# Value matrices dealt out between score products, and the next batch's right factors put behind a pair's additions

## The chip, the cores and the metric

The kernel runs on one core of one Trainium2 chip. The metric is the time of one execution in microseconds (us) on the device, as the median of several runs. A profile of one further execution shows each engine's instructions: TensorE (PE, with its weight loads as PEld), VectorE (DVE), ScalarE (ACT), GpSimd (POOL) and the queue of SyncE (SP), which issues most of the transfers.

## What is computed

A gated block of cross attention and feed-forward, in float32. `x` is 4 x 1024 x 512, the context 4 x 64 x 512; 16 heads of 64.

```python
def _L0_xattn_ref(query, key, value, w_q, w_k, w_v, w_o):
    q = split_heads(query @ w_q)
    k = split_heads(key @ w_k)
    v = split_heads(value @ w_v)
    scores = jnp.einsum('bhqd,bhkd->bhqk', q, k) * SCALE
    mask = (k_pos[None, :] <= q_pos[:, None])
    scores = scores + (1.0 - mask)[None, None, :, :] * -10000.0
    weights = jax.nn.softmax(scores, axis=-1)
    out = jnp.einsum('bhqk,bhkd->bhqd', weights, v)
    return out.transpose(0, 2, 1, 3).reshape(...) @ w_o

x = x + tanh(g_xattn) * _L0_xattn_ref(_layernorm(x), ctx, ctx, w_q, w_k, w_v, w_o)
x = x + tanh(g_ffn) * _L0_ffn_ref(_layernorm(x), w_gate, w_up, w_down)
```

The feed-forward part (`_L0_ffn_ref`) multiplies by weights of 4 bits and quantizes its activations to 16 bits; it follows the attention in the kernel, and the change does not touch it.

## The kernel before

**Tiling.** The 4096 tokens are 32 tiles of 128 rows. Two tiles make a *pair* q, so there are 16 pairs, four for each of the four batches. The kernel folds weights together ahead of the pairs. For each batch, `m_all[b]` is w_q times the batch's keys, 512 x 1024 (two parts), so that scores are one matrix product of the normalized tokens with `m_all[b]`. The *value matrix* `vwo[b]` is the batch's values times w_o times tanh(g_xattn), 1024 x 512 (two parts of four head pairs), so that the attention's output is one product of the softmax weights with `vwo[b]`.

**Seven products.** A pair's scores, and its attention, are each computed as a 2 x 2 block product with seven block products in place of eight. This needs sums of blocks of the left operand (for scores: `score_left`, four DVE additions on `xs`; for attention: the end of `weights_turned`, four on `eT`), and sums of blocks of the right operand: `batch_sums(b, k)`, four DVE operations of 128 x 1024, with k = 0 for the scores (`m_all`) and k = 1 for the attention (`vwo`). `batch_sums` is a generator with a `yield` after the second and after the fourth operation. The results of the seven products are added together from the PSUM banks by DVE and ACT.

**Stages up to the pairs.** In the first block (pool `su`, five PSUM banks `ps_mm`), keys are projected, then for each of eight head pairs `hp` w_q is turned and `m_all` made (L478 to L505), with the value projection in every second step (L507). The statistics of the first layer norm are taken there too. In the last of the eight steps the left factors of pair 0 are made (L482: `centred`, which normalizes two tiles on ACT as `xn`, and `score_left`, which transposes them on PE, copies them to `xs` on ACT and adds on DVE). Then comes the value stage (L527 to L547): 32 value matrices of 128 x 512, eight for each batch, each from two matmuls of 64 x 64 against 512 columns into one bank, and each scaled out of PSUM, by ACT for batches 0 and 2 (L543) and by DVE for 1 and 3 (L545). Batches 2 and 3 come first and are written to DRAM by POOL's queue (L547), since the 20 shared buffers `slot` cannot hold everything; between the two halves stands `batch_sums(0, 0)`.

**The pairs.** In the second block (three banks `ps_s` for scores, two `ps_o` for the attention, three `ps_tr` for transposes), L731 to L734 make pair 0's scores (`scores(0)`, with pair 1's left factors after its sixth product), its softmax and `batch_sums(0, 1)`. Each step q of the loop at L735 then makes the scores of pair q + 1, with calls put between the seven products (`between`, keyed by the product's number; the products run in the order 1, 6, 2, 5, 7, 3, 4), then softmax of pair q + 1, and last the attention of pair q (`attend`, products in the order 1, 6, 2, 7, 5, 4, 3). One `turn()` transposes the softmax weights of one of pair q's two tiles; for pair 0 both turns stand after the whole of pair 1's scores and softmax (L758), for later pairs they stand between the score products. After `attend`, in the second and fourth pair of a batch, the right factors of the next batch are made (L777), then norms (L782 to L788), and one or two weight blocks of the feed-forward are dequantized (L791).

**What sets the order.** In the second block, PE's instructions are issued in the order of the program (`manual_schedule`, L553). All other engines, and PE in the first block, follow an order made ahead of the run by a list scheduler: it takes the operation that is earliest in the program among those that it reckons to be ready by its own costs, and `high_priority(SOON)` moves an operation 150 places forward. So an operation late in the program can run early if its engine is reckoned free, and one early in the program goes first where both are ready. The order is fixed when the program is built; in the run each engine goes through its list.

Of the kernel before, what the change touches and what calls it, by code (L numbers as in the profile page):

```python
# [7 lines left out]
F32 = mybir.dt.float32  # L8
# [3 lines left out]
AF = mybir.ActivationFunctionType  # L12
# [5 lines left out]
P = 128  # L18
# [9 lines left out]
def kernel(  # L28
# [335 lines left out]
    def batch_sums(b, k):  # L364
# [21 lines left out]
        nc.vector.tensor_tensor(t4, b21, t2, sub)  # L386
        yield

    with tc.tile_pool(name="su", bufs=1) as su, tc.tile_pool(
        name="ps_mm", bufs=5, space=PSUM  # L390
    ) as ps_mm:
# [86 lines left out]
        for hp in range(HP):  # L478
            if hp + 1 < HP:
                query_turned(hp + 1)  # L480
            else:
                left[0] = score_left(0, centred(0))  # L482
            for h2 in range(HC // 2):
                two = [
                    ps_mm.tile([P, 2, CT], F32, name=f"ps_m{hp}_{h2}_{j}", tag="mm")
                    for j in range(2)
                ]
                for i in range(2):
                    hc = 2 * h2 + i
                    for j in range(2):  # L490
                        half = slice(j * D, (j + 1) * D)
                        nc.tensor.matmul(
                            two[j][:, i, :],
                            wqT[hp // 4][half, hp % 4, hc * P : (hc + 1) * P], kT[half, hp, :],
                            start=True, stop=True,
                        )
                for j in range(2):
                    for b in range(B):
                        at = (hp % 4) * P + (j if b % 2 == 0 else 1 - j) * D
                        dst = m_all[b][hp // 4][:, 2 * h2 : 2 * h2 + 2, at : at + D]  # L500
                        src = two[j][:, :, b * KL : (b + 1) * KL]
# [18 lines left out]
            for k in range(2):  # L520
                nc.gpsimd.dma_start(out=m_d[b][k], in_=m_all[b][k])


        for b in range(B):
            vwo.append([slot([P, HP // 2, H], f"vwo{b}_{n}") for n in range(2)])
        load_group(1)
        for a in reversed(range(B // 2)):  # L527
            if a == 0:
                for _ in batch_sums(0, 0):
                    pass  # L530
            for hp in range(HP):
                for b in (2 * a, 2 * a + 1):
                    ps = ps_mm.tile([P, H], F32, name=f"ps_vo{b}_{hp}", tag="mm")
                    for j in range(2):
                        half = slice(j * D, (j + 1) * D)
                        to = j if b % 2 == 0 else 1 - j
                        nc.tensor.matmul(
                            ps[to * D : (to + 1) * D, :], vT[half, hp, b * KL : (b + 1) * KL],
                            wo[hp // 4][half, hp % 4, :], start=True, stop=True,
                        )  # L540
                    dst = vwo[b][hp // 4][:, hp % 4, :]
                    if b % 2 == 0:
                        nc.scalar.activation(dst, ps, AF.Copy, scale=tanh_g[0])  # L543
                    else:
                        nc.vector.tensor_scalar(dst, ps, tanh_g[0], None, ALU.mult)  # L545
                    if b > 1 and hp % 4 == 3:
                        nc.gpsimd.dma_start(out=vwo_d[b][hp // 4], in_=vwo[b][hp // 4])  # L547


    xT = [None] * NTB  # L550
    with tc.tile_pool(name="ps_s", bufs=1, space=PSUM) as ps_s, tc.tile_pool(
        name="ps_o", bufs=1, space=PSUM
    ) as ps_o, tc.manual_schedule(engines={mybir.EngineType.PE}):  # L553

        def scores(q, between):

            a, b = left.pop(q), right[0][q // QPB]
            e = pa.tile([P, 2, NH, KL], F32, name=f"e{q}", tag="e")
            c = e.rearrange("p i (n h) k -> p i n (h k)", n=2)
            bank = {  # L560
                k: ps_s.tile([P, H], F32, name=f"{k}{q}", tag=k) for k in ("sp", "sq", "sn")
            }
            m1, c12, c22 = c[:, 1, 0], c[:, 0, 1], c[:, 1, 1]
            for k, at, start, dst, other in (
                (1, "sp", True, m1, None), (6, "sq", True, c12, m1), (2, "sp", False, c[:, 0, 0], None),
                (5, "sn", True, c22, m1), (7, "sq", False, c22, c22), (3, "sn", False, c12, c12),
                (4, "sq", False, m1, m1),
            ):
                for h in range(HC // 2):
                    nc.tensor.matmul(  # L570
                        bank[at], a[k][:, h, :], b[k][:, h, :],
                        start=start and h == 0, stop=h == HC // 2 - 1, skip_group_check=True,
                    )
                with tc.high_priority(SOON):
                    if other is None:
                        nc.scalar.copy(dst, bank[at])
                    else:
                        nc.vector.tensor_tensor(dst, bank[at], other, add)
                if k in between:
                    between[k]()  # L580
            return e

        def softmax(q, e):

            for i in range(2):
                t = 2 * q + i
                ei = e[:, i]

                if t % TPB == 0:
                    nc.vector.tensor_tensor(  # L590
                        ei, ei, cmask.unsqueeze(1).to_broadcast([P, NH, KL]), ALU.add
                    )
                mx = pa.tile([P, NH], F32, name=f"mx{t}", tag="mx")
                nc.vector.tensor_reduce(mx, ei, AX.X, ALU.max)
                sm = pa.tile([P, NH], F32, name=f"sm{t}", tag="sm")
                if q == 0:

                    nc.vector.tensor_tensor(
                        ei, ei, mx.unsqueeze(2).to_broadcast([P, NH, KL]), ALU.subtract
                    )  # L600
                    nc.scalar.activation(ei, ei, AF.Exp)
                    nc.vector.tensor_reduce(sm, ei, AX.X, ALU.add)
                else:
                    nc.vector.tensor_scalar(mx, mx, -1.0, None, ALU.mult)  # L604
                    for h in range(NH):
                        nc.scalar.activation(  # L606
                            ei[:, h, :], ei[:, h, :], AF.Exp, bias=mx[:, h : h + 1],
                            accum_out=sm[:, h : h + 1],
                        )
                rs = pa.tile([P, NH], F32, name=f"rs{t}", tag="rs")  # L610
                nc.vector.reciprocal(rs, sm)
                nc.vector.tensor_tensor(
                    ei, ei, rs.unsqueeze(2).to_broadcast([P, NH, KL]), ALU.mult
                )

        def weights_turned(q, e):

# [21 lines left out]
        def attend(q, a):  # L639
# [15 lines left out]
            for k, at, start, dst in (  # L655
# [9 lines left out]
                with tc.high_priority(SOON):  # L665
                    if k == 1:
                        nc.scalar.copy(r, bank[at])
                    else:
                        nc.vector.tensor_tensor(dst, bank[at], dst, add)  # L669

                if k == 6:
                    nc.vector.tensor_tensor(x1[:, RIGHT], x1[:, RIGHT], r, add)
# [832 lines left out]
```

## Time and profile before

| | |
|---|---|
| median of the runs shown (3 runs, 1468.91 to 1469.15) | 1469.0 us |
| the profiled execution, whole | 1467.07 us |
| its span in the profile | 1465.3 us |
| first score product of pair 0 starts | 82.06 us |
| attention of pair 0 ends, scores of pair 2 start | 130.93 us |
| attention of the last pair (15) ends | 551.37 us |
| granted PE clock over the span | 0.995 |

A row of the timeline gives the start and the length in us, the engine, the line of the program, the operation, the tile that is written and those that are read, the shape, the count of merged instructions, and in brackets the idle time of the engine before it and who ended it. One matmul in float32 appears as two records, so a score product of two matmuls is `x4` and an attention product of four is `x8`. Rows of PE overlap by some 0.2 us; the distance of two starts is what a product takes. The tile names are the program's: `xn` and `xs` for left factors of scores, `e` for scores and softmax weights, `eT` for turned weights, `sp`, `sq`, `sn` and `opn`, `oq` for banks, `xg` for a group of four token tiles to which the attention is added in place, `vb` and `mb` for a batch's value and score matrices fetched back from DRAM.

### The profile page before, as it was taken

How to read it: one execution, taken by the hardware profiler on the slowest of the kernel's cores; microseconds unless marked ns; L12 is line 12 of the kernel's file. 1: busy time of each engine (PE TensorE's matmuls, PEld its weight loads, DVE VectorE, ACT ScalarE, POOL GpSimd, SP SyncE). 2: the span in 40 equal slices, each digit the busy share in tenths (PEclk: the TensorE clock that was granted, in tenths of full speed). 3: DMA queues.
4: the chain of work that ended last, by engine and by line, in shares of the span. 5: the costliest groups of instructions: out<-in, count | busy, mean ns of one | idle time of the engine just before them, and what ended most of it. 6: DMA issues, size and time to landing. Idle time of an engine off the chain costs nothing. (4 is left out here: it accounts for less than half of the span.)

```text
span 1465.3 us, 15463 instructions
## 1 busy us (share of the span) xinstructions
PE 1417.2 (97%) x5040; PEld 869.3 (59%) x5040; DVE 1128.0 (77%) x2059; ACT 693.4 (47%) x1746; POOL 96.6 (7%) x191
## 2 busy tenths in 40 slices
PE   8898999999999998999999999999999899999999
PEld 6545766766676674444444444444444448888887
DVE  2976887977988779899956569988888897666632
ACT  2645867767678673111000049977776532222200
POOL 0100000000000001000000000000000101111110
PEclk9999999999999999999999999999999999999999
DMA  9630231431312133664322439958557475554321
GB/s 330 244 130 15 72 115 72 159 129 58 130 47 110 46 130 158 236 223 187 129 86 102 157 127 345 373 216 316 212 210 267 164 282 174 187 187 172 143 72 43
DMA packets 74168, 240.12 MB, mean 164 GB/s; under 512 B 7396, under 2 KB 7652, under 8 KB 68068
## 3 DMA queue, kind: packets, MB, share of 16 engines
q1 hardware_dynamic: 48612, 137.39, 26.8%
q0 software_dynamic: 18560, 76.56, 13.4%
q10 hardware_dynamic: 6912, 25.17, 4.3%
q8 instruction: 39, 0.64, 0.2%
q14 instruction: 45, 0.37, 0.1%
HBM read 130.03 MB, written 109.05 MB: 163 GB/s over the span
## 5 line engine op out<-in xcount | busy, mean ns | idle before, releaser
L606 ACT ACTIVATE e<-e,mx 128x64 f32<-128x64 f32 x480 | 159.7, 339 | 2.2 <-DVE mx L604 2.1
L839 PE MATMUL pqup<-t,wuT 128*128 128x512 f32 x192 | 92.3, 603 | 5.2 <-DVE raw_up L860 2.6
L606 ACT ACTIVATION_READ_ACCUMULATOR e<-e,mx 128x1 f32 x480 | 92.3, 192 | 0.0
L839 PE MATMUL pqgate<-t,wgT 128*128 128x512 f32 x192 | 90.2, 592 | 0.0
L855 ACT COPY raw_gate<-ppgate 128x512 f32<-128x512 f32 x24 | 14.0, 585 | 145.5 <-PE ppgate L839 145.5
L1372 PE MATMUL ep<-wdT,upe 128*128 128x256 f32 x336 | 77.1, 379 | 0.0
L1298 ACT ACTIVATE uie<-upe,inv_up 128x1024 int16<-128x1024 f32 x48 | 53.8, 1145 | 45.8 <-DVE upe L1302 28.7
L661 PE MATMUL oq<-t,eT 128*128 128x256 f32 x256 | 63.7, 393 | 12.0 <-DVE xg L669 8.1
L1372 PE MATMUL eq<-tw,upe 128*128 128x256 f32 x312 | 72.4, 379 | 0.0
L1372 PEld LDWEIGHTS ep<-wdT,upe 128*128 128x128 f32 x336 | 63.8, 190 | 9.1 <-issue 0.5
L1071 ACT ACTIVATE gi<-gt,inv_gate 128x1024 int16<-128x1024 f32 x48 | 54.9, 1143 | 30.3 <-DVE q L1081 30.0
L839 PEld LDWEIGHTS pqup<-t,wuT 128*128 128x128 f32 x192 | 34.7, 189 | 57.0 <-issue 29.7
L839 PE MATMUL ppgate<-xh,wgT 128*128 128x512 f32 x144 | 67.7, 592 | 0.0
L839 PE MATMUL ppup<-xu,wuT 128*128 128x512 f32 x144 | 67.7, 592 | 0.0
L1372 PEld LDWEIGHTS eq<-tw,upe 128*128 128x128 f32 x312 | 59.3, 190 | 8.1
L839 PEld LDWEIGHTS pqgate<-t,wgT 128*128 128x128 f32 x192 | 36.3, 190 | 46.1 <-issue 37.9
L1302 DVE SCALAR_TENSOR_TENSOR upe<-uie,inv_o,gse 128x1024 f32<-128x1024 int16 (+1 forms) x50 | 60.4, 1231 | 3.3 <-ACT uie L1298 3.0
L661 PEld LDWEIGHTS oq<-t,eT 128*128 128x128 f32 x256 | 49.4, 195 | 21.9 <-DVE xg L669 11.0
L570 PE MATMUL sq<-t,xs 128*128 128x512 f32 x128 | 60.3, 593 | 0.0
L629 ACT COPY eT<-ps_e 128x512 f32<-128x512 f32 x64 | 34.3, 588 | 53.5 <-PE ps_e L627 53.5
L967 DVE TENSOR_REDUCE am_gate<-raw_gate 128x1 f32<-128x1024 f32 x48 | 58.2, 1213 | 0.9
L1103 ACT ACTIVATE ar<-raw_up 128x1024 f32<-128x1024 f32 x46 | 48.2, 1047 | 19.1 <-DVE raw_up L1029 19.1
(353 smaller groups left out, 3141.2 us busy)
## 6 DMA issues: line engine op xcount, KB each, us to landing
gate_d<-raw_gate ACTq DMA_DIRECT2D x48, 512.0 KB, 2.6
gt<-gate_d SPq DMA_DIRECT2D x48, 512.0 KB, 4.8
upe<-up_d SPq DMA_DIRECT2D x24, 1024.0 KB, 5.9
up_d<-raw_up POOLq DMA_DIRECT2D x46, 512.0 KB, 3.5
gse<-gsi_d SPq DMA_DIRECT2D x24, 512.0 KB, 4.6
gsi_d<-q SPq DMA_DIRECT2D x44, 256.0 KB, 4.0
xg<-in_x_dram SPq DMA_DIRECT2D x8, 1024.0 KB, 5.2
x_d<-xg POOLq DMA_DIRECT2D x32, 256.0 KB, 2.3
```

Source lines behind the costliest of these rows:

```text
L570: nc.tensor.matmul(bank[at], a[k][:, h, :], b[k][:, h, :], start=start and h == 0, stop=h == HC // 2 - 1, skip_group_check=True,)
L606: nc.scalar.activation(ei[:, h, :], ei[:, h, :], AF.Exp, bias=mx[:, h : h + 1], accum_out=sm[:, h : h + 1],)
L629: nc.scalar.copy(eT[:, 2 * i + k], ps)
L661: nc.tensor.matmul(bank[at], a[k][:, h, :], b[k][:, h, :], start=start and h == 0, stop=h == HP // 2 - 1, skip_group_check=True,)
L839: nc.tensor.matmul(bank[at], a[k][:, h, :], b[k][:, h, :], start=start and h == 0, stop=h == HC // 2 - 1, skip_group_check=True,)
L855: nc.scalar.copy(r0[:, 0, :], bank["pp"])
L967: nc.vector.tensor_reduce(am_gate[:, u : u + 1], rf, AX.X, ALU.max, apply_absolute_value=True)
L1071: nc.scalar.activation(gi, g, AF.Copy, scale=inv_g)
L1103: nc.scalar.activation(ar, raw[u], AF.Abs)
L1298: nc.scalar.activation(ui, up[:, i, :], AF.Copy, scale=inv_u)
L1302: ins = nc.vector.scalar_tensor_tensor(o[:, i, w], ui[:, w], c_o, gs[:, i, w], ALU.mult, ALU.mult)
L1372: nc.tensor.matmul(bank[at], a[u // 2][k][:, u % 2, q % 2, :], w_of[u // 2][k][:, u % 2, :], start=start and u == 0, stop=u == UPB - 1, sk ...
```

## The change

Three things are done.

1. **Value stage.** Only batches 2 and 3 are made there, in one loop over head pairs; ACT evicts twelve of the sixteen matrices and DVE four. `batch_sums(0, 0)` now stands ahead of that loop, and pair 0's left factors in it (at `hp == 2`) rather than in the last projection step.
2. **Pairs 0 and 1.** The eight value matrices of batch 0 are made two at a time after the products 6, 2, 5 and 7 of `scores(0)`; those of batch 1 after the products 1, 6, 2 and 5 of `scores(1)`. They use the two banks of `ps_o`, and ACT evicts all of them. Pair 1's left factors (`next_left(1)`) move from between the products of `scores(0)` to after `softmax(0)`. `batch_sums(0, 1)` is split: its first two operations stand before `softmax(0)`, its last two after `softmax(1)`. Pair 0's two turns move from after `softmax(1)` to after the products 3 and 4 of `scores(1)`, and pair 2's left factors from after product 3 to after product 4.
3. **Later batches.** `attend` returns its last addition, and the four operations of `batch_sums(b + 1, ...)` in the pairs 1, 3, 5, 7, 9 and 11 are placed on DVE's list behind it (`issue_after`).

`scores` and `softmax` move out of the second block with their bodies as they were, but that `scores` gets its three banks as an argument.

```diff
@@ L386: moved here from the second block @@
+    def scores(q, between, banks):
...
+        bank = dict(zip(("sp", "sq", "sn"), banks))
...
@@ L478, in the last projection step @@
             if hp + 1 < HP:
                 query_turned(hp + 1)
-            else:
-                left[0] = score_left(0, centred(0))
...
@@ L527, the value stage @@
-        for a in reversed(range(B // 2)):
-            if a == 0:
-                for _ in batch_sums(0, 0):
-                    pass
-            for hp in range(HP):
-                for b in (2 * a, 2 * a + 1):
...
-                    if b % 2 == 0:
-                        nc.scalar.activation(dst, ps, AF.Copy, scale=tanh_g[0])
-                    else:
-                        nc.vector.tensor_scalar(dst, ps, tanh_g[0], None, ALU.mult)
-                    if b > 1 and hp % 4 == 3:
-                        nc.gpsimd.dma_start(out=vwo_d[b][hp // 4], in_=vwo[b][hp // 4])
+        for _ in batch_sums(0, 0):
+            pass
+        def value_matrix(b, hp, ps):
...
+            if b != B - 1 or hp % 2 == 0:
+                nc.scalar.activation(dst, ps, AF.Copy, scale=tanh_g[0])
+            else:
+                nc.vector.tensor_scalar(dst, ps, tanh_g[0], None, ALU.mult)
+
+        for hp in range(HP):
+            if hp == 2:
+                left[0] = score_left(0, centred(0))
+            for b in range(2, B):
+                value_matrix(b, hp, ps_mm.tile([P, H], F32, name=f"ps_vo{b}_{hp}", tag="mm"))
+                if hp % 4 == 3:
+                    nc.gpsimd.dma_start(out=vwo_d[b][hp // 4], in_=vwo[b][hp // 4])
@@ L555, the second block @@
+        def score_banks(q):
+            return [ps_s.tile([P, H], F32, name=f"s{k}_{q}", tag=f"s{k}") for k in range(3)]
+
+        values_done = [0, 0]
+
+        def values_of(b, n):
+
+            def some():
+                for _ in range(n):
+                    hp = values_done[b]
+                    values_done[b] += 1
+                    value_matrix(
+                        b, hp, ps_o.tile([P, H], F32, name=f"ps_vo{b}_{hp}", tag=("opn", "oq")[hp % 2])
+                    )
+            return some
@@ L669, attend @@
-                        nc.vector.tensor_tensor(dst, bank[at], dst, add)
+                        ins = nc.vector.tensor_tensor(dst, bank[at], dst, add)
...
             finished(2 * q, x1)
+            return ins.ins
@@ L730 @@
         two = centred(1)
-        ahead = scores(0, {3: lambda: next_left(1)})
+        ahead = scores(0, dict.fromkeys((6, 2, 5, 7), values_of(0, 2)), score_banks(0))
+        firsts = batch_sums(0, 1)
+        next(firsts)
         softmax(0, ahead)
-        for _ in batch_sums(0, 1):
-            pass
+        next_left(1)
@@ L752 @@
-                behind = {3: lambda: next_left(q + 2)}
-                if q > 0:
-                    behind = {5: turn, 3: lambda: (a.append(turn()), next_left(q + 2))}
-                ahead = scores(q + 1, behind)
+                behind = {5: turn, 3: lambda: (a.append(turn()), next_left(q + 2))}
+                if q == 0:
+                    behind = {**dict.fromkeys((1, 6, 2, 5), values_of(1, 2)), 3: turn, 4: behind[3]}
+                ahead = scores(q + 1, behind, score_banks(q + 1))
                 softmax(q + 1, ahead)
-            if q == 0 or q + 1 == NQ:
+            if q == 0:
+                next(firsts)
+            if q + 1 == NQ:
                 turn()
                 a = [turn()]
@@ L776 @@
-            attend(q, a[0])
-            if b + 1 < B and k in (1, QPB - 1):
-                for _ in batch_sums(b + 1, k // 2):
-                    pass
+            added = attend(q, a[0])
+            with tc.issue_after(added):
+                if b + 1 < B and k in (1, QPB - 1):
+                    for _ in batch_sums(b + 1, k // 2):
+                        pass
```

More of the change, by code (lines that the diff above doesn't have):

```diff
@@ L387, in batch_sums @@
         yield
+    def scores(q, between, banks):
+        a, b = left.pop(q), right[0][q // QPB]
+        e = pa.tile([P, 2, NH, KL], F32, name=f"e{q}", tag="e")
+        c = e.rearrange("p i (n h) k -> p i n (h k)", n=2)
+        bank = dict(zip(("sp", "sq", "sn"), banks))
+        m1, c12, c22 = c[:, 1, 0], c[:, 0, 1], c[:, 1, 1]
+        for k, at, start, dst, other in (
+            (1, "sp", True, m1, None), (6, "sq", True, c12, m1), (2, "sp", False, c[:, 0, 0], None),
+            (5, "sn", True, c22, m1), (7, "sq", False, c22, c22), (3, "sn", False, c12, c12),
+            (4, "sq", False, m1, m1),
+        ):
+            for h in range(HC // 2):
+                nc.tensor.matmul(
+                    bank[at], a[k][:, h, :], b[k][:, h, :],
+                    start=start and h == 0, stop=h == HC // 2 - 1, skip_group_check=True,
+                )
+            with tc.high_priority(SOON):
+                if other is None:
+                    nc.scalar.copy(dst, bank[at])
+                else:
+                    nc.vector.tensor_tensor(dst, bank[at], other, add)
+            if k in between:
+                between[k]()
+        return e
@@ new lines, in softmax @@
+    def softmax(q, e):
+        for i in range(2):
+            t = 2 * q + i
+            ei = e[:, i]
+            if t % TPB == 0:
+                nc.vector.tensor_tensor(
+                    ei, ei, cmask.unsqueeze(1).to_broadcast([P, NH, KL]), ALU.add
+                )
+            mx = pa.tile([P, NH], F32, name=f"mx{t}", tag="mx")
+            nc.vector.tensor_reduce(mx, ei, AX.X, ALU.max)
+            sm = pa.tile([P, NH], F32, name=f"sm{t}", tag="sm")
+            if q == 0:
+                nc.vector.tensor_tensor(
+                    ei, ei, mx.unsqueeze(2).to_broadcast([P, NH, KL]), ALU.subtract
+                )
+                nc.scalar.activation(ei, ei, AF.Exp)
+                nc.vector.tensor_reduce(sm, ei, AX.X, ALU.add)
+            else:
+                nc.vector.tensor_scalar(mx, mx, -1.0, None, ALU.mult)
+                for h in range(NH):
+                    nc.scalar.activation(
+                        ei[:, h, :], ei[:, h, :], AF.Exp, bias=mx[:, h : h + 1],
+                        accum_out=sm[:, h : h + 1],
+                    )
+            rs = pa.tile([P, NH], F32, name=f"rs{t}", tag="rs")
+            nc.vector.reciprocal(rs, sm)
+            nc.vector.tensor_tensor(
+                ei, ei, rs.unsqueeze(2).to_broadcast([P, NH, KL]), ALU.mult
+            )
@@ L526 @@
         load_group(1)
-        for a in reversed(range(B // 2)):
-            if a == 0:
-                for _ in batch_sums(0, 0):
-                    pass
-            for hp in range(HP):
-                for b in (2 * a, 2 * a + 1):
[L533 to L541, printed above, removed]
-                    if b % 2 == 0:
-                        nc.scalar.activation(dst, ps, AF.Copy, scale=tanh_g[0])
-                    else:
-                        nc.vector.tensor_scalar(dst, ps, tanh_g[0], None, ALU.mult)
-                    if b > 1 and hp % 4 == 3:
-                        nc.gpsimd.dma_start(out=vwo_d[b][hp // 4], in_=vwo[b][hp // 4])
+        for _ in batch_sums(0, 0):
+            pass
+        def value_matrix(b, hp, ps):
+            for j in range(2):
+                half = slice(j * D, (j + 1) * D)
+                to = j if b % 2 == 0 else 1 - j
+                nc.tensor.matmul(
+                    ps[to * D : (to + 1) * D, :], vT[half, hp, b * KL : (b + 1) * KL],
+                    wo[hp // 4][half, hp % 4, :], start=True, stop=True,
+                )
+            dst = vwo[b][hp // 4][:, hp % 4, :]
+            if b != B - 1 or hp % 2 == 0:
+                nc.scalar.activation(dst, ps, AF.Copy, scale=tanh_g[0])
+            else:
+                nc.vector.tensor_scalar(dst, ps, tanh_g[0], None, ALU.mult)
[6 more added lines that the diff above has]
+                    nc.gpsimd.dma_start(out=vwo_d[b][hp // 4], in_=vwo[b][hp // 4])
     xT = [None] * NTB
@@ L553 @@
     ) as ps_o, tc.manual_schedule(engines={mybir.EngineType.PE}):
[L555 to L572, printed above, removed]
-                    )
[L574 to L614, printed above, removed]
@@ L752 @@
                 a = []
-                behind = {3: lambda: next_left(q + 2)}
-                if q > 0:
-                    behind = {5: turn, 3: lambda: (a.append(turn()), next_left(q + 2))}
-                ahead = scores(q + 1, behind)
+                behind = {5: turn, 3: lambda: (a.append(turn()), next_left(q + 2))}
+                if q == 0:
+                    behind = {**dict.fromkeys((1, 6, 2, 5), values_of(1, 2)), 3: turn, 4: behind[3]}
+                ahead = scores(q + 1, behind, score_banks(q + 1))
                 softmax(q + 1, ahead)
-            if q == 0 or q + 1 == NQ:
+            if q == 0:
+                next(firsts)
+            if q + 1 == NQ:
                 turn()
```

## The prediction

> **What bounds the kernel now.** I read the page first, then the waits of TensorE (PE), then busy times by stage, then the timelines of the stages with waits.
>
> ```profile
> PE 1417.2 (97%) x5040; PEld 869.3 (59%) x5040; DVE 1128.0 (77%) x2059; ACT 693.4 (47%) x1746; POOL 96.6 (7%) x191
> ```
>
> PE is busy for 97% of the span. Only two things can shorten it: fewer matmuls, or fewer waits of PE. The change removes no matmul, so the question is which of PE's waits it ends and which it makes. The next view sums the waits of PE from 56 to 440 us: who waited for whom, us in total, times, the longest.
>
> ```profile
> PE oq L661 <- DVE xg L669: 5.1, 4, 2.9
> PE oq L661 <- DVE eT L634: 3.8, 1, 3.8
> PE ps_xn L352 <- ACT xn L340: 2.8, 2, 2.3
> PE ps_e L627 <- DVE e L612: 2.8, 2, 1.9
> PE ps_vo L537 <- DVE vwo L545: 2.1, 3, 0.7
> PE sp L570 <- DVE vwo L545: 0.9, 1, 0.9
> ```
>
> All but the first belong to the stretch from 56 to 119 us, which the first part of the change rewrites; the first belongs to the later pairs, where the second part acts. By stage (stretch, its length, then busy us of PE, PEld, DVE, ACT, POOL, then the granted clock):
>
> ```profile
> 51.92:63.72 11.80, 9.02 (x57) 6.63 (x57) 10.73 (x43) 8.51 (x30) 0.85 (x2) 1.00 0.33 125
> 63.72:82.06 18.34, 15.21 (x130) 5.61 (x129) 16.69 (x28) 11.58 (x17) 2.32 (x5) 1.00 0.84 344
> 82.06:93.31 11.25, 11.25 (x33) 5.46 (x34) 2.75 (x5) 1.41 (x3) 0.00 (x0) 1.00 0.26 95
> 93.31:113.09 19.78, 17.00 (x59) 8.43 (x58) 19.78 (x26) 10.50 (x16) 0.00 (x0) 1.00 0.18 53
> 113.09:130.93 17.84, 14.04 (x58) 11.74 (x57) 13.03 (x26) 11.92 (x67) 0.54 (x1) 0.90 0.00 0
> ```
>
> Row two is the value stage: DVE is busy 16.7 of 18.3 us, since it evicts half of the 32 value matrices and makes batch 0's right factors. Row three is pair 0's scores: DVE works only 2.75 of 11.25 us. Row four is pair 1's scores with pair 0's softmax: DVE has no free moment. So DVE idles in one stage and holds PE up in the stages on both sides of it. Row five, pair 0's attention, shows a clock of 0.90. PE's rows there, and in two later pairs:
>
> ```profile
> 118.78 2.71 PE L661 MATMUL oq<-t,eT 128*128 128x256 f32 x8 [3.80 <-DVE eT L634]
> 121.28 2.90 PE L661 MATMUL opn<-vwo,eT 128*128 128x256 f32 x8
> ...
> 324.74 3.65 PE L661 MATMUL oq<-t,eT 128*128 128x256 f32 x8 [2.86 <-DVE xg L669]
> ...
> 442.55 1.99 PE L661 MATMUL oq<-t,eT 128*128 128x256 f32 x8 [2.86 <-DVE xg L669]
> ```
>
> An undisturbed attention product has 1.89 and the next starts 1.73 later. After the wait of 3.80 the following two starts come 0.77 and 1.02 late; after one wait of 2.86 the next start is 1.75 late, after the other about 0.1.
>
> **The part up to pair 0's first product (82.06).** (a) Making pair 0's left factors moves from the last projection step into the value loop. The two waits for xn, 2.29 and 0.49, should go: the projection's matmuls no longer stand behind them. -2.78. The eight transposes and four DVE sums move along unchanged. (b) 16 of the 32 value matrices leave. Two of them take 0.86 in the undisturbed run (PEld starts at 65.49, 66.35, 67.21), so 0.43 each: -6.88. (c) Batch 0's four right-factor sums (1.21 each, 1.13 apart) now come ahead of the value loop, and DVE evicts 4 matrices there instead of 16. The waits for DVE's evictions, three of 0.7 and one of 0.95, should go: -3.07. (d) What is late next is ACT: it evicts 12 of the 16 matrices at 0.69, 8.28, and has vT's copy (0.59) and two xs copies (1.08 together): 9.95, against 6.88 + 1.2 = 8.1 on PE. +1.9. If centred rows of pair 1 also fall here (1.52 for two), it is +3.4; if the evictions overlap as the xs copies do (0.50 apart), nothing. Pair 0's first product then starts at 82.06 - 2.78 - 6.88 - 3.07 + 1.9 = 71.2 (bounds 69.3 and 73).
>
> **From that product to the end of pair 0's attention (130.93, that is 48.87 later).** (e) The 16 matrices return in eight groups of two: +6.88. No row shows one between score products; the nearest, the change from projection to value matrices at 63.72, has no gap, so I take 0 for the switch and keep 0.1 a group (0.8) as the other bound. ACT evicts all of them into two banks of ps_o, at least a product (1.72) apart for each group; ACT is busy 1.41 of 11.25 there, so this hides. (f) DVE gets 6.88 more time, and two of the four value-side sums (2.3) move into its idle stage. The waits for e (0.86 and 1.90) and eT (3.80) should go, and with them the late starts (0.77 and 1.02): -8.35. (g) New waits. Pair 1's left factors are now issued after softmax 0, so the four DVE sums (0.34 apart) stand behind its long operations; in the trace of before they were ready at 94.37 and the first two done at 96.85. PE needs two of them 2.6 us after the transposes (one product, two matrices). Softmax 0 has on DVE a mask addition, two maxima, two subtractions (1.13 each), 5.6 in all; if the sums fall between them, PE waits 1 to 3 us; if behind the sums and normalizations also (some 5 more), about 8.5. I take 2.5, since in the trace DVE's list slips short operations between long dependent ones (94.37 and 96.44 do just that). (h) The second turning of pair 0's weights comes after the last score product, and only next_left (0.87) and one product (1.73) cover two copies (1.07) and two DVE sums (1.3), while the second half of the value-side sums (2.3) must be done before the fourth product. I take 1.5 (bounds 0 and 4). Sum: 48.87 + 6.88 - 8.35 + 2.5 + 1.5 = 51.4, so the attention ends at 122.6 instead of 130.93: **-8.3**.
>
> This is where a rule of the skill speaks against the change. The rows above show that a wait of 1.90 leaves the next products at full pace, and that waits of 2.86 and 3.80 can cost 1.8 more. The Trainium skill (TensorE: Matmul & The Clock Gate, "Part 1: The HAM clock gate") says that the array falls to half its clock after an idle window of about 3.4 us, free-running. By that page a new wait in (g) above its window would be followed by up to one window at half pace, an estimate of 1.7 us more. By the rows alone the price is 0 to 1.8, from a wait of 2.86 on. My 2.5 stays below that; the rival with 8.5 pays the 1.8 of the rows.
>
> **The right factors of the next batch (pairs 1, 3, 5, 7, 9, 11).** Four DVE operations of 1.21 are held until the pair's last addition. In the trace they sit in the middle of the attention, as here at 440:
>
> ```profile
> 439.20 1.23 DVE L612 TENSOR_TENSOR e<-e,rs 128x1024 f32<-128x1024 f32 x1
> 440.34 0.68 DVE L675 TENSOR_TENSOR xg<-xg,r 128x512 f32<-128x512 f32 x1
> 440.95 1.22 DVE L381 TENSOR_TENSOR t<-vb 128x1024 f32<-128x1024 f32 x1
> 442.08 0.42 DVE L669 TENSOR_TENSOR xg<-oq,xg 128x256 f32<-128x256 f32 x1
> ```
>
> L669 is the addition that frees the bank for the product that waited 2.86. Of this wait the sum L381 is 1.13; the rest is statistics, a normalization and L675, which stay. At pairs 7, 9 and 11 (waits 2.86, 1.75, 2.86) one operation goes from ahead of the addition: 3 x 1.13 = 3.4; pairs 3 and 5 lose waits of 0.2 and 0.26 and the two late starts with them: 0.8. **-4.2**; bounds: -11 (all six pairs fall to 27.63, the pitch of pair 4, from 26.95+28.09+28.16+32.41+29.64+30.76 less 0.87 in pair 1), and 0. What is queued behind the held operations on DVE is the pair's norm and the next pair's turned-weight sums; PE needs the norm's result at the xn transposes, 12 us into the next pair (after pair 7, the offsets were done 6.0 us in, at 335.98). Held operations add at most 4.6: 10.6. So I cost this at nothing.
>
> **Sum.** 1467.07 (1465.3 of span, 1.8 around it) - 8.3 - 4.2 = 1454.6. The median of the runs is 1469.0, 1.9 above the profiled one; -12.5 on it gives **1456.5**, own range 1449 to 1462.
>
> **Rivals.** *All waits go*: 69.3 + 48.87 + 6.88 - 8.35 = 116.7, -14.2, and -8 to -11 at the later pairs: 1469 - 23 = **1446**. For it: DVE's 8.5 idle us in pair 0's scores. Against: new waits (g) and (h) are built in. *Left factors behind all of softmax 0*: 8.5 + 1.8 in place of 2.5, so 1456.5 + 7.8 = **1464**. For it: they are issued behind it, and DVE was full there. Against: DVE's list fills gaps. *Held sums become the bound* (slower): in the pair after a held batch DVE has 25.39 busy of 27.63 (pair 4) or 27.72 of 28.13 (pair 10); 3.4 more is over the pitch, and the normalization of the next weights, ahead of PE's first turning, comes late. It decides when the six places cost more than the 8.3 of the first part, 1.4 each; at 2.3 each, half of the four operations, it is 13.8 - 8.3: **1474.5**. Against it: the sums leave the pair before, which then has that much room, and two dequantizations per pair can wait. *The reordering does nothing*: DVE and ACT follow a list made ahead, whose order may trade one wait for another; then 1469.
>
> **Chances.** Forecast 0.60, all waits go 0.12, left factors late 0.12, nothing 0.05, held sums 0.11. A measurement of this kernel tells 0.2% (2.9 us) from no change. The first three are faster: 0.84; same 0.05; slower 0.11. The range 1446 to 1467 takes in the forecast, the late left factors and half of the best case.
>
> **What would show it.** Right: score products of pair 0 start near 71 and its attention ends near 122; no xn wait at 56; eT and e waits gone; one new wait of the second product of pair 1 on xs; at pairs 7, 9, 11 an oq wait shorter by about 1.1, and L381 after the last L669. Wrong: a start after 74, a wait on xs above 5, waits of ps_e or ps_xn in the pairs after 1, 3, 5, 7, 9, 11.

## The result and the profile after

| | before | after |
|---|---|---|
| median of the runs | 1468.96 us (1468.91 to 1469.15) | 1519.87 us (1518.19 to 1520.52) |
| span in the profile | 1465.3 us | 1516.4 us |
| first score product of pair 0 | 82.06 us | 72.83 us |
| attention of pair 0 ends | 130.93 us | 132.39 us |
| attention of pair 15 ends | 551.37 us | 600.72 us |

The kernel became slower: the ratio is 1.0347, with a 95% interval of 1.0334 to 1.036. The forecast was 1456.5, with a range up to 1467. Of the added 50.9 us, 1.5 had come up when pair 0's attention ended; the rest comes later. The page after, its line of busy times and its line of granted clocks:

```profile
PE 1440.0 (95%) x5040; PEld 876.5 (58%) x5040; DVE 1122.8 (74%) x2047; ACT 700.6 (46%) x1758; POOL 96.6 (6%) x191
...
PEclk9999999998979799899999999999999999999999
```

The count of matmuls is the same. PE's busy time rose by 22.8 us (from 1417.2) and its idle time by 28.3 (51.1 - 22.8): PE both waited longer and ran longer on the same work. In the second line, each digit is the clock in tenths over 37.9 us; the first 8 and the two 7 (slices from 341, 417 and 493 us) show three places; the second 8, from 607, lies behind the pairs. The waits of PE over the whole run of the changed kernel (who waited for whom, us in total, times, the longest):

```profile
PE ps_xm L716 <- ACT xm L703: 34.1, 3, 11.5
PE ps_xn L352 <- ACT xn L340: 5.8, 3, 2.1
PE oq L676 <- DVE xg L684: 5.0, 4, 1.9
...
PE s L403 <- DVE xs L357: 2.2, 1, 2.2
```

The first line is new. `xm` are the renormed token tiles, made by ACT with the norm's offsets and transposed by PE into `xT` for the feed-forward part. It waited three times, 11.4 on average. The third line fell from 8.4 (six times) before to 5.0: this is the wait that the held sums were to shorten. The waits of `ps_e` for `e` and of `oq` for `eT`, 2.8 and 3.8 before, are gone.

The lengths of the loop's steps place it (us, from PE's timelines). Step q begins with the first score product of pair q + 1 and ends with pair q's attention; step 0 here also has pair 0's own scores.

| step | 0 | 1 | 2 | 7 | 8 | 9 | 10 | 11 | 12 |
|---|---|---|---|---|---|---|---|---|---|
| before | 48.87 | 26.95 | 28.01 | 32.41 | 27.63 | 29.64 | 28.13 | 30.76 | 27.63 |
| after | 59.56 | 26.75 | 27.69 | 29.82 | 43.97 | 28.64 | 46.12 | 29.82 | 45.55 |

Two things happened: step 0 grew by 10.69 and ate the 9.23 that its start had gained; steps 8, 10 and 12 grew by 16.3, 18.0 and 17.9, 52.2 together. These steps follow the held sums at 7, 9 and 11. The steps after the other three held places (2, 4 and 6) grew by 0.7 at most.

Step 8 on PE after:

```profile
345.93 0.60 PE L716 MATMUL ps_xm<-ident,xm 128*128 128x128 f32 x4
358.02 1.11 PE L716 MATMUL ps_xm<-ident,xm 128*128 128x128 f32 x4 [11.50 <-ACT xm L703]
358.93 3.62 PE L676 MATMUL opn<-vb,eT 128*128 128x256 f32 x8
362.34 2.13 PE L676 MATMUL oq<-t,eT 128*128 128x256 f32 x8
```

The first tile of the pair is transposed, the second one waits 11.50 for ACT, and since PE goes in program order, the whole attention stands behind it. The first attention product then has 3.62 in place of 1.89, and the next start comes 3.41 later in place of 1.73: half pace. The granted clock is 0.50 in this stretch (358.93 to 362.34) and 1.00 again from 366.04. ACT in the same step:

```profile
340.48 0.81 ACT L703 ACTIVATE xm<-xg,off,rstd 128x512 f32<-128x512 f32 x1 [1.36 <-DVE off L185]
...
345.60 0.35 ACT L439 ACTIVATE e<-e,mx 128x64 f32<-128x64 f32 x1
...
357.17 0.80 ACT L703 ACTIVATE xm<-xg,off,rstd 128x512 f32<-128x512 f32 x1
```

ACT was not waiting for anything: between 345.60 and 357.17 it did the 32 exponentials of the next softmax, with two copies between them, and the second `xm` came after them in its list. Before, both stood ahead of them:

```profile
335.95 0.81 ACT L687 ACTIVATE xm<-xg,off,rstd 128x512 f32<-128x512 f32 x1
...
339.89 0.81 ACT L687 ACTIVATE xm<-xg,off,rstd 128x512 f32<-128x512 f32 x1
...
349.31 0.35 ACT L606 ACTIVATE e<-e,mx 128x64 f32<-128x64 f32 x1
```

And DVE after, from the first of the held sums (L381) to the norm's last operation (L185):

```profile
330.26 1.22 DVE L381 TENSOR_TENSOR t<-vb 128x1024 f32<-128x1024 f32 x1
...
334.92 1.22 DVE L386 TENSOR_TENSOR t<-vb,t 128x1024 f32<-128x1024 f32 x1
...
336.65 0.16 DVE L172 TENSOR_SCALAR ve_b<-mv 128x4 f32<-128x4 f32 x1
...
340.28 0.24 DVE L185 SCALAR_TENSOR_TENSOR off<-mv,rstd 128x4 f32<-128x4 f32 x2
```

The norm goes from L172 to L185. One of its two first operations was done before the sums (at 324.74); the other, for the statistics that come last, stands behind all four of them, and the offsets are done 11.55 us into the step (340.52 - 328.97). Before it was 6.03 (335.98 - 329.95):

```profile
335.75 0.23 DVE L185 SCALAR_TENSOR_TENSOR off<-mv,rstd 128x4 f32<-128x4 f32 x2
```

Step 0 after, PE's first products and groups of two value matrices:

```profile
76.43 1.93 PE L591 MATMUL ps_vo<-wo_sb,vT 64*64 64x512 f32 x8
78.30 1.98 PE L403 MATMUL s<-m_all,xs 128*128 128x512 f32 x4
80.21 1.93 PE L591 MATMUL ps_vo<-wo_sb,vT 64*64 64x512 f32 x8
...
100.46 1.98 PE L403 MATMUL s<-t,xs 128*128 128x512 f32 x4 [2.17 <-DVE xs L357]
```

A group of two matrices keeps PE for 1.87 (76.43 to 78.30), where the prediction had 0.86, and a score product followed by a group has 1.91 (78.30 to 80.21), not 1.72. For eight groups the two differences sum to 9.6. The first three rows show no wait: PE was busy. The wait of 2.17 is for the left factors.

### The profile page after: what moved, and what is told of

It reads as the page before. It is cut to its first block, busy times and chain, and to the rows that moved or that the text cites. A ratio compares the mean times of both kernels' runs of the same rounds, so it can differ in the third digit from the quotient of the medians.

```text
span 1516.4 us, 15480 instructions
## 1 busy us (share of the span) xinstructions
PE 1440.0 (95%) x5040; PEld 876.5 (58%) x5040; DVE 1122.8 (74%) x2047; ACT 700.6 (46%) x1758; POOL 96.6 (6%) x191
## 5 line engine op out<-in xcount | busy, mean ns | idle before, releaser
L411 DVE TENSOR_TENSOR e<-s,e 128x512 f32<-128x512 f32 x80 | 55.0, 688 | 71.6 <-PE s L403 71.2
L403 PE MATMUL s<-t,xs 128*128 128x512 f32 x192 | 93.5, 610 | 2.2 <-DVE xs L357 2.2
L1320 ACT ACTIVATE uie<-upe,inv_up 128x1024 int16<-128x1024 f32 x48 | 53.7, 1145 | 46.7 <-DVE upe L1324 28.3
L409 ACT COPY e<-s 128x512 f32<-128x512 f32 x32 | 18.7, 584 | 98.0 <-PE s L403 97.9
L861 PEld LDWEIGHTS pqgate<-t,wgT 128*128 128x128 f32 x192 | 36.3, 190 | 46.1 <-issue 37.9
L403 PE MATMUL s<-m_all,xs 128*128 128x512 f32 x128 | 59.7, 598 | 1.2 <-DVE vwo L599 0.9
L403 PEld LDWEIGHTS s<-t,xs 128*128 128x128 f32 x192 | 35.9, 195 | 42.9 <-issue 39.9
```

Source lines behind the costliest of these rows:

```text
L403: nc.tensor.matmul(bank[at], a[k][:, h, :], b[k][:, h, :], start=start and h == 0, stop=h == HC // 2 - 1, skip_group_check=True,)
L861: nc.tensor.matmul(bank[at], a[k][:, h, :], b[k][:, h, :], start=start and h == 0, stop=h == HC // 2 - 1, skip_group_check=True,)
L1320: nc.scalar.activation(ui, up[:, i, :], AF.Copy, scale=inv_u)
```

## The experiments

Three questions were open: which part of the change costs the 52 us, by what way the held sums delay ACT, and why two value matrices take 1.87.

**One part alone, and the other.** The first kernel is the kernel before with the third part alone; the second is the changed kernel without it.

```diff
-            added = attend(q, a[0])
-            with tc.issue_after(added):
-                if b + 1 < B and k in (1, QPB - 1):
-                    for _ in batch_sums(b + 1, k // 2):
-                        pass
+            attend(q, a[0])
+            if b + 1 < B and k in (1, QPB - 1):
+                for _ in batch_sums(b + 1, k // 2):
+                    pass
```

(This is the second; the first makes the opposite edit in the kernel before.)

> The kernel before with only the third part of the change: the next batch's sums behind the pair's last addition. Theory A (the held sums make the norm late, and ACT then takes the second renormed tile after 32 exponentials): pairs 8, 10 and 12 take 44 to 46 us each instead of 27.6 to 28.1, pairs 3, 7, 9 and 11 gain some 5 together, so 1510 to 1518. Rival (the dealt-out first part has upset the order of the later pairs): no wait of ps_xm on xm, 1460 to 1469.

Measured: 1520.72 us (2 runs), ratio 1.0364 (1.0334 to 1.0394). Steps 8, 10 and 12 have 43.48, 45.87 and 43.83, and the wait of `ps_xm` for `xm` is 34.3 in three times. The time lies 2.7 above theory A's range: this had counted on 5 us gained in the steps 3, 7, 9 and 11, and in the trace they gained 1.7 together.

> The changed kernel without the third part: the sums stand where the list puts them. Theory A: pairs 8, 10, 12 at 27.6 to 28.2, oq waits of 2 to 3 us at pairs 7, 9 and 11 are back, pair 0's attention ends at 132.4 as in the changed kernel: 1467 to 1473. Rival (first part at fault): the waits of ps_xm on xm stay, 1505 to 1516.

Measured: 1470.03 us (8 runs), ratio 1.0009 (0.9996 to 1.0022). No wait of `ps_xm` for ACT; steps 8 and 12 have 27.63 again. Step 0 has 59.55. So the third part alone makes the whole loss, and the first two parts come out at nothing: what the start gains, step 0 gives back.

**The held sums behind the norm.** In the changed kernel, the same block stands after the calls of `norm_of` in place of before them. The sums are still held until the pair's last addition.

> The changed kernel with the held sums issued after the norm instead of before it; still held behind the last addition. Theory A: the norm is early again, no wait of ps_xm on xm, pairs 8, 10, 12 at 27.6 to 30, while pairs 7, 9 and 11 keep their gain: 1464 to 1471. Rival (the pair after a held batch is full on DVE, whatever the order): pairs 8, 10, 12 stay above 35 us, 1490 or more.

Measured: 1468.7 us (8 runs), ratio 1.0006 (0.9995 to 1.0017). Steps 8, 10 and 12 have 27.63, 29.87 and 27.62. The norm's second L172 now slips in ahead of the last sum, at 335.20, the offsets are done 8.96 into step 8, and on ACT both `xm` are ahead of the exponentials:

```profile
338.61 0.81 ACT L703 ACTIVATE xm<-xg,off,rstd 128x512 f32<-128x512 f32 x1 [0.29 <-DVE off L185]
...
340.75 0.80 ACT L703 ACTIVATE xm<-xg,off,rstd 128x512 f32<-128x512 f32 x1
...
349.05 0.35 ACT L439 ACTIVATE e<-e,mx 128x64 f32<-128x64 f32 x1
```

The loss of 51 us is gone by the order of the program alone, with the same operations; step 10 keeps 1.8 us for waits of PE for `xn` (29.87 against 28.13 before). Against the kernel without the third part, the wait of `oq` for `xg` has 5.0 in place of 8.3; the stretch from pair 0's attention to the end of pair 15 is 418.6 in place of 423.3 in the traces; the medians differ by 1.3, which is less than single runs of one kernel do.

**The order on ACT alone.** The held sums stay ahead of the norm, as in the change, and only `xm`'s place on ACT is moved forward:

```diff
-                nc.scalar.activation(
-                    xn, xg[g][:, i, :], AF.Identity, bias=off2[:, t : t + 1],
-                    scale=rstd2[:, t : t + 1],
-                )
+                with tc.high_priority(SOON):
+                    nc.scalar.activation(
+                        xn, xg[g][:, i, :], AF.Identity, bias=off2[:, t : t + 1],
+                        scale=rstd2[:, t : t + 1],
+                    )
```

> The changed kernel, held sums still ahead of the norm on VectorE, but ScalarE's second renormed tile of a pair is placed ahead of the exponentials in its list. Theory A (the 11.5 us waits of pairs 8, 10 and 12 are ScalarE's order: 32 exponentials stand ahead of the tile that TensorE needs): those pairs come back from 43.97, 46.12 and 45.55 us to 28 to 32 each, the wait of ps_xm for xm falls from 34.1 to under 6, and the whole to 1469 to 1480. Rival B (VectorE is simply full after the held sums, so that the norm would be late in any order): the pairs stay at 38 us or more and the whole at 1500 or more.

Measured: 1481.08 us (2 runs), ratio 1.0083 (1.0064 to 1.0101), a little over theory A's bound, and far from theory B's 1500. Steps 8, 10 and 12 have 32.23, 32.62 and 30.63. PE in step 8:

```profile
345.81 1.82 PE L352 MATMUL ps_xn<-ident,xn 128*128 128x128 f32 x8 [2.54 <-ACT xn L340]
347.42 3.07 PE L403 MATMUL s<-t,xs 128*128 128x512 f32 x4
350.33 1.04 PE L717 MATMUL ps_xm<-ident,xm 128*128 128x128 f32 x8
```

The long wait is gone, though the norm is as late as in the change: the offsets are done 11.54 into step 8, and on ACT the second `xm` (344.23) is ahead of the exponentials (348.40). What stays, 12.4 us against the kernel with the norm first, is mainly the norm's own lateness: PE waits 2.54 for the next `xn`, and runs at half pace for some products behind it. Part of it comes from the edit, for the second `xm` now stands ahead of `xn`, and this wait was 1.83 in the change. So, by the medians, the loss of 51.2 divides into 38.8 that went with ACT's order (1519.87 - 1481.08) and 12.4 that stayed (1481.08 - 1468.7).

**Value matrices batch by batch.** The code of `value_matrix` suggests why a group is slow. The two matmuls of one matrix use the array's rows and columns (0, 0) and (64, 64) in an even batch and (0, 64) and (64, 0) in an odd one: `to = j if b % 2 == 0 else 1 - j`. The loop before alternated the batches, so neighbours used different quarters of the array; a group of the change has two matrices of one batch, on the same two quarters. The kernel before, with this edit alone:

```diff
-            for hp in range(HP):
-                for b in (2 * a, 2 * a + 1):
+            for b in (2 * a, 2 * a + 1):
+                for hp in range(HP):
```

> The kernel before with the value loop turned: eight matrices of one batch, then eight of the next, so that neighbours use the same two quarters of the array. Theory C (a matrix uses two of four quarters; only neighbours of an even and an odd batch run together): two neighbours take 1.72 us instead of 0.86, the 32 matrices 27.5 instead of 13.8, the value stage grows by 8 to 11 us: 1477 to 1480. Rival (the 1.0 us more per group in the changed kernel is a cost of changing between products of 128 rows and of 64): stage as before, 1468 to 1471.

Measured: 1474.17 us (3 runs), ratio 1.0045 (1.0022 to 1.0068). The value stage is one row without a gap (the second row is pair 0's first product):

```profile
65.85 23.00 PE L537 MATMUL ps_vo<-wo_sb,vT 64*64 64x512 f32 x128
89.70 1.98 PE L570 MATMUL sp<-m_all,xs 128*128 128x512 f32 x4 [0.85 <-DVE vwo L545]
```

ACT's evictions in it start 0.86 apart, one matrix each, where the kernel before needed 0.86 for two. The stage has 23.85 in place of 18.34. It is less than twice as long, as the stage before also held 2.1 of waits for DVE and some neighbours at the border of two batches still overlapped. The loss, 5.7 against the kernel before as run beside it (1468.46), lies under the expected 8 to 11, but the rate is what the theory says. (The profiled execution, the slowest of the three, is 8.9 longer than that of before; 2.1 of this had come up ahead of the value stage.)

**Groups of one head pair of both batches.** The kernel with the norm first, and each group made of matrices that use different quarters:

```diff
...
-                for _ in range(n):
-                    hp = values_done[b]
-                    values_done[b] += 1
-                    value_matrix(
-                        b, hp, ps_o.tile([P, H], F32, name=f"ps_vo{b}_{hp}", tag=("opn", "oq")[hp % 2])
-                    )
+            hp = next(heads)
+            for b in range(2):
+                value_matrix(b, hp, ps_o.tile([P, H], F32, name=f"ps_vo{b}_{hp}", tag=("opn", "oq")[b]))
...
```

Batch 0's value matrices are now complete only in pair 1's scores, so all four sums of `batch_sums(0, 1)` stand behind these, ahead of pair 1's softmax.

> The kernel of the run that gave 1468.7 (held sums behind the norm), with each group of two value matrices made of one head pair of both batches instead of two head pairs of one batch; both batches' first sums then stand behind pair 1's scores. Theory C (two matrices run beside each other only when they use different quarters of the array): a group takes 0.9 to 1.1 us instead of 1.87, the attention of pair 0 is 59.55 - 4 = 55 to 56.5, and the whole is 1460 to 1463, unless the later first sums of batch 1 make a wait at the first tail, which would show as a wait of PE there and give up to 4 back. Rival (a group costs its switch from and to the score products, whatever its matrices): groups stay at 1.7 or more and the whole at 1467 to 1470.

Measured: 1467.33 us (10 runs), ratio 0.9995 (0.9984 to 1.0007). The time looks like the rival's, the rows do not:

```profile
77.42 1.09 PE L591 MATMUL ps_vo<-wo_sb,vT 64*64 64x512 f32 x8
78.44 1.98 PE L403 MATMUL s<-m_all,xs 128*128 128x512 f32 x4
...
97.28 2.58 PE L403 MATMUL s<-t,xs 128*128 128x512 f32 x4 [2.23 <-DVE xs L357]
...
121.31 2.72 PE L671 MATMUL oq<-t,eT 128*128 128x256 f32 x8 [3.24 <-DVE t L382]
```

A group has 1.02 (77.42 to 78.44), so the theory of the quarters holds, and 8 x 0.85 = 6.8 left step 0. It came back in two places. The first attention product with a sum waits 3.24 for it, and the next two starts come 0.8 and 1.0 late: 5.0. And the wait for `xs`, there in the changed kernel too, is now followed by late starts, 1.5. Step 0 has 59.65, and it starts at 73.81, 1.06 later than in the kernel with the norm first; why is not shown. The expectation had allowed 4 for this wait, not the late starts.

**Left factors ahead of softmax 0.** As the kernel with groups of both batches, with `next_left(1)` called after pair 0's last score product, inside `scores(0)`:

> As the run with groups of both batches, and batch 1's left factors are queued inside pair 0's scores, ahead of its softmax. If the 2.17 us wait of the scores s for xs is the left factors standing behind the softmax on VectorE, it goes, and the time is 1.5 to 2.5 less than that run's. If it is the product's own lateness, the wait stays and so does the time.

Measured: 1464.98 us (10 runs), ratio 0.9979 (0.9969 to 0.9988); 2.35 less than the kernel with both batches, and the wait of `s` for `xs` L357 is gone from the list of waits; one of 0.69 for an eviction of a value matrix came up near its place. Step 0 has 57.0. So the wait for `xs` was the left factors' place behind the softmax.

**Six groups in pair 0's scores, two in pair 1's.** As the kernel with the left factors ahead, and the four sums of `batch_sums(0, 1)` follow one product behind the last group:

```diff
-        ahead = scores(0, {**dict.fromkeys((6, 2, 5, 7), values_of_both), 4: lambda: next_left(1)}, score_banks(0))
+        ahead = scores(0, {**dict.fromkeys((1, 6, 2, 5, 7, 3), values_of_both), 4: lambda: next_left(1)}, score_banks(0))
...
-                    behind = {**dict.fromkeys((1, 6, 2, 5), values_of_both), 3: turn, 4: behind[3]}
+                    behind = {
+                        **dict.fromkeys((1, 6), values_of_both), 2: lambda: [*batch_sums(0, 1)],
+                        3: turn, 4: behind[3],
+                    }
```

> As the run before it, with six of the groups in pair 0's scores and two in pair 1's, and batch 0's first two sums right behind the second of them. If a wait for these sums costs the runs before it something, it goes here: 1457 to 1461. If they cost nothing, this run equals them within 1 us.

Measured: 1460.12 us (5 runs, 1458.62 to 1461.87), ratio 0.9938 (0.9924 to 0.9951): faster than both kernels. Step 0 has 52.73, with PE's longest wait in it 1.14, and pair 0's attention ends at 126.26, 4.67 ahead of the kernel before. The product that had waited 3.24 now reads:

```profile
115.80 1.99 PE L671 MATMUL oq<-t,eT 128*128 128x256 f32 x8 [0.34 <-DVE eT L644]
```

The profiled execution, its slowest (1461.87), has a span of 1460.1, 5.2 less than before, while the medians of the two kernels, run side by side, differ by 8.4; the two numbers differ by no more than the single runs do.

## Why the prediction was wrong

**The step that failed** is the last of the part on the right factors: "PE needs the norm's result at the xn transposes, 12 us into the next pair ... Held operations add at most 4.6: 10.6. So I cost this at nothing." The size was nearly right: 6.0 + 4.6 gave 10.6, and the offsets came at 11.55. The cover was wrong, twice. First, PE does not need the offsets but what ACT makes of them, and ACT's share was left out: in step 8, `xm`, two copies and `xn` lie between the offsets (340.52) and the transposes of `xn` (343.01), 2.5 us where 1.4 were reckoned to be left. This is the late norm: 12.4 us stayed when only ACT's order was put right, 10.4 of it in steps 8, 10 and 12, with the half pace behind the waits. Second, and larger, ACT has a list of its own, made ahead. With the held sums ahead of the norm, the second `xm` stands behind 32 exponentials on this list. A delay of 5.5 us on DVE (offsets at 6.03 and at 11.55 of step 8) thus became one of 18.3 on ACT (9.94 and 28.20 into the step), and cost 38.8 us of the whole. The prediction knew both that the order is made ahead and that a held operation delays what is behind it on DVE, but followed the delay only along DVE to PE, and never asked what ACT's list does with it.

The rival that held sums become the bound had the right sign, and its place (the steps after 7, 9 and 11, among six) but not its way: it asked whether DVE has room for 3.4 us more, and named the normalization of the next weights. DVE was busy 26.77 of the 43.97 us of step 8, and with the norm first the same step takes 27.63, with DVE busy for 24.19; room was not short. The rival that the reordering does nothing named the way, a list made ahead that trades one wait for another, but priced the trade at nothing. Of the signs of being wrong that the prediction gave, one came: waits of `ps_xn` in the steps 8, 10 and 12. The larger waits, of `ps_xm`, were not among them.

**Its other steps.**

- (a) to (d), the start: 71.2 predicted, 72.83 measured, within the bounds of 69.3 to 73. The waits for `xn` went; a wait of 1.23 for `m_all` took part of their place. Of the waits for DVE's evictions, the three of 0.7 went and the one of 0.95 ahead of the first product stayed.
- (e), the eight groups, was mis-sized: +6.88 predicted, and 0.8 for the switches as a bound; measured 8 x 1.87 = 15.0 and 8 x 0.19 = 1.5. The figure of 0.43 a matrix came from rows in which an even and an odd batch alternate, and it holds for such neighbours only (1.02 for two in the later kernels). The difference, 9.6, turned the -8.3 of the first part into +1.5.
- (f), the waits for `e` and `eT` and their late starts: gone, as predicted.
- (g), the left factors behind softmax 0: 2.5 predicted, 2.17 measured. Moving them ahead brought 2.35.
- (h), the turns and the second half of the value-side sums: 1.5 predicted, 0.41 measured.
- From these, 122.6 + 1.63 + 9.6 - 0.33 - 1.1 = 132.4, and 132.39 was measured: with the rate of the matrices put right, the sum for step 0 closes.
- The held sums' gain: -4.2 predicted. The waits of `oq` for `xg` at pairs 7, 9 and 11 fell from 2.86, 1.75 and 2.86 to 1.93, 0.74 and 1.92: 2.9 together where 3.4 had been worked out, and the short ones at pairs 3 and 5 (0.20 and 0.26) went. In time it is less certain, since each of these waits may be followed by half pace or not: from pair 0's attention to pair 15's end, the traces have 420.4 before, 418.6 with the norm first and 420.3 in the fastest kernel.

**What stays open.** Why the list scheduler puts the second `xm` behind the exponentials in steps 8, 10 and 12 and not in 2, 4 and 6 was not settled. In steps 8, 10 and 12 the norm covers 8 columns (ACT's square root has 128x8 in step 8, 128x4 in step 4) and takes in the next group of tiles; that this makes the difference is argued, not shown. A late norm alone is not enough: in step 4 after the change the offsets come 11.44 into the step, nearly as late as in step 8, and both `xm` (225.94 and 228.56) stay ahead of the exponentials. There PE's next `xn` did not wait for this norm; in step 8 it did.

## What to carry to other kernels

An operation that is moved delays its followers, and where the other engines go through lists made ahead, the delay must be followed into every list: look which long block stands beside the operations that depend on it, for here a slip of 5 us past the edge of a block of 12 cost the block. The price of a matmul that uses part of the array holds only for the neighbours that it had in the trace; before moving it, look at which rows and columns those used. A wait that has been worked out should be costed to the engine that needs the last result, with every engine on the way counted.

## What the runs showed of the hardware

Matmuls of 64 x 64 ran side by side on different quarters of the array, and one after the other on the same: 1.02 for a group of two matrices against 1.87, with the same number of instructions. The Trainium skill (TensorE: Matmul & The Clock Gate, "Part 3: Packing small matmuls — row/col tiling") says that matmuls smaller than the array can run concurrently in it, each with a tile position of its own; the traces agree for different quarters, at 0.43 to 0.51 a matrix against 0.86 to 0.94.

Half pace came after shorter waits than the rows of before had shown. In the fastest kernel, at step 7:

```profile
318.42 2.53 PE L671 MATMUL oq<-t,eT 128*128 128x256 f32 x8 [1.93 <-DVE xg L679]
320.74 3.09 PE L671 MATMUL opn<-vwo,eT 128*128 128x256 f32 x8
```

A wait of 1.93 is followed by two products of 2.53 and 3.09, against 1.89 undisturbed, and the granted clock is 0.78 and 0.59 in them. At the same place in the changed kernel, a wait of 1.93 was followed by full pace (1.99). The wait of 2.17 in the changed kernel was followed by full pace (1.98, the length of an undisturbed score product there), the one of 2.23 in the kernel with both batches by half pace. The wait of 2.29 for `xn` in the last projection step was followed by full pace in the kernel before (a granted clock of 1.00 from 56.21 to 60.07) and by a slower one in the kernel batch by batch (0.65 from 57.32 to 62.20). So in these runs the length of a single wait does not decide it. The same skill page (section "Part 1: The HAM clock gate") puts the idle window at about 3.4 us, free-running; a wait of 1.93 that is followed by half pace lies well below this figure. Whether idle time earlier than the wait counts too is not shown.
